# The output projection's bias: from a matrix product on TensorE to an addition on GpSimd

## The chip, the cores and the metric

The kernel runs on one core of a Trainium2 chip. A core has five engines, each with its own queue of instructions that it works off in order: TensorE (PE, matrix products; PEld is its loading of weights), VectorE (DVE), ScalarE (ACT), GpSimd (POOL) and SyncE (SP, which here issues the DMAs). PE writes to PSUM, eight banks of memory beside it; GpSimd works on SBUF, the main on-chip memory. The metric is the device time of one execution in microseconds (us), the median of several.

## The reference

Four sequences of 2048 tokens with 256 channels pass through four layers, each added to its input:

```python
x = x + _L0_attn_a_ref(_layernorm(x, axis=-1), ...)   # row 1 of the sequence times W, plus b, for all tokens
x = x + _L0_ffn_ref(_layernorm(x, axis=-1), ...)
x = x + _L0_attn_b_ref(_layernorm(x, axis=-1), ...)   # 16 heads of 64, window of 128 tokens back, RoPE
x = x + _L0_ffn_ref(_layernorm(x, axis=-1), ...)
```

The FFN is `sigmoid(xr @ W_r) * (relu(xk @ W_k)**2 @ W_v)`, where `xr` and `xk` mix each token with the one before it. The windowed attention ends in

```python
return merged @ Wo.T + bo
```

and it is this `bo`, 256 numbers that are the same for every token, that the change is about.

## The kernel before, in words

Tokens are worked off in 32 groups of 256 (`g`), two tiles `j` of 128 tokens each (128 partitions); eight groups make a sequence. A group passes through the stages load (`x`), first FFN (`f0`), normalisation for attention (`ln`), values (`v0` to `v3`), queries and keys of four quads of heads (`q0` to `q3`), attention of the four quads (`s0` to `s3`), output projection (`o`), second FFN (`f1`; the last group's is cut into two halves, `f1` and `f2`) and store (`sv`). A stage is a list of steps. Each line of such a list (`SPEC`, for instance lines 1127 to 1135) names a step, its engine (`p` PE, `v` DVE, `s` ACT, `g` POOL, `q` a DMA on SP) with an assumed duration, the steps it needs, the buffers it takes and the buffers it gives back.

A planner (`Plan`, line 143) turns these lists into one order before the program is built. It plays the steps through on the assumed durations; whenever an engine is free, it takes among the steps that could begin within 0.3 us of the earliest the one with the lowest rank. A rank is group times 44 plus a number from the table `RANK` (line 51), plus an extra number for the first five and the last five groups. The table's numbers come from a search. The order is fixed by this: the engines work off their queues as issued (`_Engine`, line 264, through whose line 276 nearly all instructions are recorded, so that most rows of the profile name that line). In the steady part, instructions of several groups stand mixed on each engine; while PE forms the first q product of one group, it finishes the output projection of the group three before it.

Values are split in a high and a low half, so that the products are exact enough in half-width numbers. For a product of tokens and weights three products run, high by high, high by low, low by high. What the change and the prediction touch:

- `Ln` (line 1126). The steps are `st` (mean and variance on DVE), `rs` (shift and scale on POOL, tiles `a_mv`, `a_rs`), `xn` (the normalised rows, on POOL, tile `a_xn`, from the tokens `x`), `hi` (ACT), `lo` (the low half, on POOL, `a_xhl`), `tr` (a transposing DMA on SP, `a_xT`). `a_xT` feeds the products for values, queries and keys.
- `Out` (line 1485). Each of `o0` and `o1` forms for one tile of 128 tokens 24 products of 128x256 (eight slices of the 1024 channels of the heads, three products each) from the transposed context (`at_ctT`) and the weights `WO`, and adds a 25th, `ones` by `bo3` (line 1513), all into one half of a PSUM bank (`po`). `ad` (for the last group the halves `b0`, `b1`) then runs on DVE: x = po * osc + x, where `osc` undoes the weights' scale.
- `bo3` (line 377) holds the scaled bias in three rows of bf16 numbers that sum to it, other rows zero, so that a product with a matrix of ones gives the bias on every row. The setup step `ob` (line 805) makes it by ten GpSimd instructions on three partitions, in the tile `tmp`. It comes after `mk`, which makes the attention mask's factors from the mask in the same tile; `lm` loads mask and bias into it.
- `Load` (line 924). Its step `a1` adds the first layer's result to the tokens on POOL (`x<-x,vb`), an instruction of 128x512 numbers.
- Setup (line 457) loads and rescales all weights, each with a few large products (`u_q`, `u_k`, `u_v`, `u_o`, sums of squares `pn_q`, `pn_k`, `pn_v`), among the first groups' first steps.

Of the kernel before, what the change touches and what calls it, by code (L numbers as in the profile page):

```python
# [8 lines left out]
BF16 = mybir.dt.bfloat16  # L9
# [9 lines left out]
P = 128  # L19
# [32 lines left out]
    "p.c1": -5056.91, "p.c2": 2969.02, "p.c3": -4885.05, "p.lv": -3111.05, "p.lb": -2925.83, "p.lw": -5009.81,  # L52
    "p.lo": -413.49, "p.lk": -2678.25, "p.lm": 2640.67, "p.lq": -3077.55, "p.fk": -1972.19, "p.fr": -2838.78,
    "p.fv": -777.00, "p.bd": -2779.47, "p.nvs": 3014.63, "p.nvm": 3072.90, "p.nvr": -2978.83, "p.nks": -788.22,
    "p.nkm": -4306.80, "p.nkr": -83.63, "p.nqs": -5037.35, "p.nqm": -4939.68, "p.nqr": -774.36, "p.sc": -472.11,
    "p.wv0": 570.16, "p.xv0": -201.89, "p.yv0": 3153.22, "p.zv0": -4686.76, "p.wv1": -2600.05, "p.xv1": -3342.91,
    "p.yv1": -610.29, "p.zv1": -4852.83, "p.wk0": -3021.86, "p.xk0": -1892.46, "p.yk0": -821.64, "p.zk0": -2369.83,
    "p.wk1": -2733.80, "p.xk1": -83.69, "p.yk1": -1953.56, "p.zk1": -2430.55, "p.wq0": -168.05, "p.xq0": 2297.47,
    "p.yq0": -4898.14, "p.zq0": -5081.41, "p.wq1": 2689.14, "p.xq1": -2913.52, "p.yq1": 3363.58, "p.zq1": -5071.63,
    "p.mk": -3071.43, "p.mu": -2906.24, "p.frh": -2530.67, "p.frl": -2423.55, "p.fkh": -2983.12, "p.fkl": 3185.31,  # L60
    "p.fvs": -769.81, "p.fvh": -4579.58, "p.fvl": 3091.15, "p.oq": -3006.79, "p.om": -204.90, "p.oc": -4648.57,
    "p.ox": -4580.42, "p.ob": -4965.08, "p.wo0": -613.03, "p.yo0": -2788.56, "p.zo0": -2882.62, "p.wo1": 3475.98,
    "p.yo1": -4703.07, "p.zo1": -4980.00, "r.ld": -5200.49, "r.st": 3455.58, "r.rs": -4687.73, "r.xn": 3456.91,
    "r.tr": 2907.19, "r.cp": -4814.90, "r.mm": 3513.18, "r.bi": -4976.56, "r.ad": -273.75, "x.ld": -4781.49,
    "x.a1": -513.94, "f0.st": -4882.63, "f0.rs": 2754.65, "f0.xn": 2986.21, "f0.tr": -4910.79, "f0.xt": -4990.79,
    "f0.hs": -3080.33, "f0.d": 2586.18, "f0.xm": -151.13, "f0.xo": -4611.65, "f0.xh": 976.57, "f0.xl": -4986.30,
    "f0.pk": -393.93, "f0.pr": -1868.76, "f0.rl": 3385.50, "f0.sq": 2308.38, "f0.kh": -5040.27, "f0.kl": -676.62,
    "f0.th": -6078.70, "f0.pv": 1034.70, "f0.sg": -4582.52, "f0.ad": 2796.64, "ln.st": -560.18, "ln.rs": -2135.71,
    "ln.xn": -358.88, "ln.hi": -845.47, "ln.lo": -4727.91, "ln.tr": -4597.42, "ln.cs": 1425.54, "tab.sc": 2955.10,
    "tab.st": -4548.65, "v0.mm": 1390.97, "v0.hi": -4851.14, "v0.lo": -952.76, "v1.mm": -2687.29,  # L70
    "v1.hi": -2644.64, "v1.lo": 2842.52, "v2.mm": 75.57, "v2.hi": -351.20, "v2.lo": -3081.42, "v3.mm": -4752.71,
    "v3.hi": -3057.25, "v3.lo": -4482.10, "q0.qm": -697.49, "q0.km": -1950.26, "q0.ka": -2699.89,
    "q0.kb": -5039.26, "q0.ad": 6.08, "q0.hi": -4974.92, "q0.lo": -5211.77, "q0.ks": -630.96, "q1.qm": -3584.31,
    "q1.km": -5189.02, "q1.ke": -5178.75, "q1.ka": -4943.18, "q1.mu": -992.72, "q1.ad": 1417.95, "q1.hi": 2888.04,
    "q1.lo": -4733.64, "q1.ks": -4326.00, "q2.qm": -468.39, "q2.km": -5058.89, "q2.ka": -2789.23,
    "q2.kb": -2972.37, "q2.ad": -2884.86, "q2.hi": 2658.83, "q2.lo": -924.24, "q2.ks": -2518.12, "q3.qm": 518.16,
    "q3.km": -4610.64, "q3.ka": 2530.62, "q3.kb": -4722.76, "q3.ad": -2764.39, "q3.hi": 2839.46, "q3.lo": -857.55,
    "q3.ks": -6086.78, "s0.k0": -1920.73, "s0.k1": -4586.15, "s0.k2": -613.21, "s0.k3": -2474.73,
    "s0.ks": -1923.23, "s0.sc": -3035.71, "s0.m0": -3099.45, "s0.m1": -3049.20, "s0.m2": -3015.22,
    "s0.m3": 2557.63, "s0.e0": -861.34, "s0.h0": -2876.34, "s0.l0": -2849.45, "s0.e1": 3370.73, "s0.h1": -2599.69,  # L80
    "s0.l1": 1349.23, "s0.t0": -2539.64, "s0.e2": 3083.70, "s0.h2": -1860.52, "s0.l2": 3055.36, "s0.e3": 2664.91,
    "s0.h3": -4879.42, "s0.l3": -610.50, "s0.t1": -4583.99, "s0.av": -4852.99, "s0.i0": 570.93, "s0.n0": -3079.20,
    "s0.ch": 2366.40, "s0.cl": -571.44, "s0.tc": -571.05, "s1.k0": -3309.12, "s1.k1": -1922.89, "s1.k2": -3002.20,
    "s1.k3": -2726.33, "s1.ks": -184.97, "s1.sc": -2823.37, "s1.m0": -2407.99, "s1.m1": -5176.15,
    "s1.m2": -1860.79, "s1.m3": 2664.46, "s1.e0": -2792.04, "s1.h0": -5036.68, "s1.l0": -5011.21,
    "s1.e1": -2759.97, "s1.h1": -2211.92, "s1.l1": -435.00, "s1.t0": -901.97, "s1.e2": 3228.18, "s1.h2": -2875.68,
    "s1.l2": -330.17, "s1.e3": -3095.98, "s1.h3": -4480.63, "s1.l3": -2400.51, "s1.t1": -40.32, "s1.av": -4976.07,
    "s1.i0": -302.67, "s1.n0": -5059.03, "s1.ch": -2945.71, "s1.cl": -4833.32, "s1.tc": -580.01, "s2.k0": -5104.06,
    "s2.k1": -2518.92, "s2.k2": -609.18, "s2.k3": -198.65, "s2.ks": -4270.64, "s2.sc": -3396.12, "s2.m0": -5359.90,
    "s2.m1": 3353.04, "s2.m2": -2954.66, "s2.m3": 2954.52, "s2.e0": -4801.17, "s2.h0": -4748.29, "s2.l0": -2533.65,  # L90
    "s2.e1": 2657.60, "s2.h1": -4876.22, "s2.l1": -143.77, "s2.t0": 3181.31, "s2.e2": -4740.23, "s2.h2": -1971.93,
    "s2.l2": -938.59, "s2.e3": 2929.40, "s2.h3": 3383.64, "s2.l3": -3250.26, "s2.t1": -4528.02, "s2.av": -3295.20,
    "s2.i0": -813.73, "s2.n0": -495.95, "s2.ch": -48.33, "s2.cl": 3091.26, "s2.tc": -696.74, "s3.k0": -677.40,
    "s3.k1": -3123.97, "s3.k2": -1933.84, "s3.k3": -465.00, "s3.ks": -4922.97, "s3.sc": -3446.85, "s3.m0": -798.61,
    "s3.m1": -4809.14, "s3.m2": 2876.12, "s3.m3": -4696.24, "s3.e0": -3417.38, "s3.h0": -4927.16,
    "s3.l0": -1999.52, "s3.e1": -4448.94, "s3.h1": -2880.18, "s3.l1": -280.82, "s3.t0": -2938.10,
    "s3.e2": -4878.66, "s3.h2": 3143.56, "s3.l2": -4964.39, "s3.e3": -4936.60, "s3.h3": -2514.89,
    "s3.l3": -1028.30, "s3.t1": -492.35, "s3.av": -2744.89, "s3.i0": 3016.46, "s3.n0": -1868.36, "s3.ch": 884.13,
    "s3.cl": -4564.07, "s3.tc": -5366.32, "o.o0": 2643.02, "o.o1": -3044.73, "o.ad": -158.89, "f1.st": 2937.82,
    "f1.rs": -2889.62, "f1.xn": 3469.38, "f1.tr": -4576.63, "f1.xt": 552.29, "f1.hs": -510.30, "f1.d": -2519.76,  # L100
    "f1.xm": 3150.42, "f1.xo": -608.94, "f1.xh": -2506.38, "f1.xl": -4708.72, "f1.pk": -1296.49, "f1.pr": 3476.81,
    "f1.rl": -5093.90, "f1.sq": -2850.79, "f1.kh": -5039.71, "f1.kl": -814.45, "f1.th": -3076.11, "f1.pv": 2685.28,
    "f1.sg": -2990.66, "f1.ad": -805.51, "sv.sv": -5172.96, "q0.kp": -272.05, "q1.kp": 3376.69, "q2.kp": -1225.68,
    "q3.kp": 3472.01, "o.b0": 1345.63, "o.b1": -2554.79, "w0.sv": 3471.29, "f2.st": -5011.19, "f2.rs": -3308.71,
    "f2.xn": -3405.13, "f2.tr": -2831.72, "f2.xt": -3325.07, "f2.hs": -2014.91, "f2.d": 1332.12, "f2.xm": 2950.21,
    "f2.xo": 2796.33, "f2.xh": 3364.00, "f2.xl": -909.62, "f2.pk": -2992.00, "f2.pr": 2885.42, "f2.rl": 539.64,
    "f2.sq": 1425.59, "f2.kh": -67.86, "f2.kl": 2844.93, "f2.th": 2905.43, "f2.pv": -5337.55, "f2.sg": 3157.44,
    "f2.ad": -4704.62, "w1.sv": 3214.41, "x!0": 280.61, "f0!0": -466.19, "ln!0": -1931.41, "tab!0": 407.32,
    "v0!0": -398.48, "v1!0": -330.74, "v2!0": -346.65, "v3!0": 347.03, "q0!0": -660.79, "q1!0": 28.80,
    "q2!0": 462.27, "q3!0": -379.97, "s0!0": 250.27, "s1!0": 1256.31, "s2!0": 655.38, "s3!0": -1508.73,  # L110
    "o!0": -1757.96, "f1!0": -2364.52, "sv!0": 2125.66, "x!1": -633.85, "f0!1": -1962.50, "ln!1": 1727.42,
    "tab!1": -240.15, "v0!1": -2055.69, "v1!1": -17.38, "v2!1": -1635.07, "v3!1": -1933.31, "q0!1": 1435.50,
    "q1!1": -913.86, "q2!1": 541.01, "q3!1": -1282.06, "s0!1": -1069.83, "s1!1": 856.98, "s2!1": -2363.56,
    "s3!1": -571.61, "o!1": 860.95, "f1!1": 519.89, "sv!1": -1291.03, "x!2": -877.71, "f0!2": -334.58,
# [1582 lines left out]
```

## Time and profile before

| what | value |
|---|---|
| median of 3 runs | 1600.59 us (1600.19 to 1601.61) |
| profiled execution, its own time | 1597.72 us |
| its span, first to last instruction | 1595.9 us |
| mean granted PE clock in it | 0.991 |
| DMA | 248.23 MB, mean 156 GB/s |
| x<-x,vb on POOL | 32, 1274 ns each |
| po<-bo,ones on PE | 64, 273 ns each, 17.4 us busy |

A row of the profile gives engine, operation, written tile <- read tiles, shape, count, then busy time and the mean duration of one in ns. Durations of products include the time until the result is through the array, and products overlap in it; how fast they follow each other is seen in a timeline, from start to start. In a timeline a row begins with start and duration in us, and ends with the time for which the engine stood idle before it and the engine and tile that it waited for. In a table by stage a row has the stretch, its length, each engine's busy time and count of instructions, the granted PE clock, the share of time that the DMA engines were busy, and GB/s.

The period of a steady group, from one group's last bias product to that of the next, is 46 to 47 us.

### The profile page before, as it was taken

The page shows a single profiled execution, that of the slowest core. Times are in us where ns is not written, and L with a number is a line of the kernel's source. Part 1 is how long each engine was busy: PE and PEld are TensorE (multiplying, and loading weights), DVE is VectorE, ACT ScalarE, POOL GpSimd, SP SyncE. Part 2 cuts the span into 40 slices and gives each one's busy share as a digit, 9 for nine tenths or more (in the row PEclk, how much of TensorE's full clock was granted, in tenths as well). Part 3 has the DMA queues.
Part 4 walks back from the last instruction along what each step waited for, and adds up shares of the span by engine and source line. Part 5 has one row for each costly group of instructions (what it writes and reads, how often), then busy time and mean ns, then how long its engine had stood idle before and what let it go on. Part 6 is the DMA issues. An engine that isn't in the chain of part 4 may idle for free.

```text
span 1595.9 us, 55776 instructions
## 1 busy us (share of the span) xinstructions
PE 1493.1 (94%) x22887; PEld 1241.3 (78%) x22888; DVE 1438.1 (90%) x2607; ACT 1345.6 (84%) x2742; POOL 1317.3 (83%) x1409
## 2 busy tenths in 40 slices
PE   7989889999999999999999999999999999999976
PEld 4767778777777887887887878788887778887765
DVE  6889898999999999999999999999999999998973
ACT  5678788888988888898988889898888989888882
POOL 6899877788888888888888889888888988888732
PEclk9999999999999999999999999999999999999997
DMA  7059998889889799989798989997878989989781
GB/s 225 11 131 168 163 175 179 153 167 157 148 160 173 164 153 163 160 170 161 159 152 152 166 165 166 169 168 166 139 149 152 181 155 173 163 164 161 147 159 34
DMA packets 858831, 248.23 MB, mean 156 GB/s; under 512 B 822736, under 2 KB 857808, under 8 KB 858576
## 3 DMA queue, kind: packets, MB, share of 16 engines
q1 hardware_dynamic: 858144, 244.66, 82.3%
q8 instruction: 179, 2.93, 0.8%
q14 instruction: 76, 0.62, 0.1%
q10 hardware_dynamic: 432, 0.01, 0.0%
HBM read 42.22 MB, written 26.21 MB: 43 GB/s over the span
## 4 chain that ended last, share of the span: by engine, by line
PE 52%; DVE 18%; ACT 17%; POOL 7%; issue 6%; DMA 1%; DVEq 0%; ACTq 0%; SPq 0%; POOLq 0%
PE qk_pd L276 11%; PE po L276 9%; PE at_s L276 8%; PE pv L276 7%; PE at_cx L276 7%; PE f_pv L276 5%; ACT at_s L276 5%; DVE qk_A L276 3%; ACT at_phl L276 3%; DVE at_phl L276 3%; DVE at_mn L276 3%; PE f_pk L276 3%; PE f_pr L276 2%; DVE qk_B L276 2%; ACT f_xh L276 2%
## 5 line engine op out<-in xcount | busy, mean ns | idle before, releaser
L276 ACT ACTIVATE at_s<-at_s,at_mn 128x256 f32<-128x256 f32 x1024 | 462.7, 452 | 27.7 <-DVE at_mn L276 11.0
L276 DVE TENSOR_TENSOR at_phl<-at_s,at_phl 128x512 f16<-128x512 f32 x512 | 346.3, 682 | 40.3 <-ACT at_phl L276 37.1
L276 POOL TENSOR_TENSOR qk_A<-qk_A,qk_B 128x512 f32<-128x512 f32 x256 | 320.9, 1277 | 44.9 <-DVE qk_B L276 43.9
L276 DVE TENSOR_REDUCE at_mn<-at_s 128x2 f32<-128x512 f32 x512 | 325.3, 680 | 3.5 <-PE at_s L276 3.2
L276 ACT CAST at_phl<-at_s 128x512 f16<-128x512 f32 x512 | 300.6, 587 | 12.8 <-DMA at_pt<-at_phl 0.4
L276 PE MATMUL at_cx<-v,at_pt 128*128 128x65 f16 x5952 | 202.6, 194 | 37.3 <-DVE qk_B L276 24.5
L276 PEld LDWEIGHTS <-at_pt 128*128 128x128 f16 x5952 | 193.8, 98 | 52.0 <-issue 48.3
L276 POOL TENSOR_TENSOR at_ct<-at_c,at_ct 128x512 f16<-128x512 f32 x128 | 149.0, 1164 | 63.0 <-ACT at_ct L276 62.7
L276 PE MATMUL at_s<-qk_k,qk_q 32*128 32x256 f16 (+1 forms) x6144 | 189.7, 264 | 0.0
L276 PE MATMUL qk_pd<-a_xT,w_q_h 128*128 128x256 f16 x1024 | 176.3, 274 | 9.3 <-DVE at_c L276 3.8
L276 POOL TENSOR_TENSOR f_xl<-f_xm,f_xh 128x1024 fp32r<-128x1024 f32 x63 | 148.7, 2360 | 40.0 <-issue 24.9
L276 PE MATMUL po<-wo_h,at_ctT 128*128 128x256 f16 x1024 | 178.0, 273 | 1.0 <-DMA at_ctT<-at_ct 1.0
L276 DVE TENSOR_TENSOR qk_A<-qk_pd,a_cs 128x1024 f32<-128x1024 f32 x128 | 156.0, 1219 | 23.6 <-PE qk_pd L276 10.1
L276 PE MATMUL qk_pd<-a_xT,w_k_h 128*128 128x256 f16 x1024 | 176.8, 275 | 0.0
L276 PE MATMUL pv<-w_v_h,a_xT 128*128 128x512 f16 x512 | 161.7, 379 | 12.2 <-DVE at_phl L276 9.4
L276 PEld LDWEIGHTS <-at_ctT 128*128 128x128 f16 x1536 | 147.9, 98 | 18.1 <-DMA at_ctT<-at_ct 1.2
L276 PEld LDWEIGHTS <-qk_q 32*128 32x128 f16 x6144 | 153.4, 93 | 6.1
L276 POOL TENSOR_TENSOR qk_k<-qk_A,qk_k 128x512 f16<-128x512 f32 x128 | 149.4, 1167 | 0.0
L276 POOL TENSOR_TENSOR qk_q<-qk_A,qk_q 128x512 f16<-128x512 f32 x128 | 149.3, 1166 | 0.0
L276 PEld LDWEIGHTS <-a_xT 128*128 128x128 f16 x768 | 71.3, 98 | 98.9 <-DVE at_phl L276 16.9
L276 PE MATMUL qk_pd<-a_xT,w_k_l 128*128 128x256 f16 x512 | 140.6, 275 | 0.0
L276 PE MATMUL qk_pd<-a_xT,w_q_l 128*128 128x256 f16 x512 | 140.1, 274 | 0.0
(195 smaller groups left out, 3866.6 us busy)
## 6 DMA issues: line engine op xcount, KB each, us to landing
qk_kd<-qk_k SPq DMA_DIRECT2D x112, 128.0 KB, 2.4
qk_k<-qk_kd SPq DMA_DIRECT2D x112, 128.0 KB, 3.1
a_cs<-csd SPq DMA_DIRECT2D x24, 384.0 KB, 3.8
x<-in_x_dram SPq DMA_DIRECT2D x32, 256.0 KB, 3.6
out_dram<-x SPq DMA_DIRECT2D x31, 256.0 KB, 2.5
at_pt<-at_phl SPq DMA_TRANSPOSE x256, 4.5
a_cs<-in_cs_dram SPq DMA_DIRECT2D x32, 96.0 KB, 3.4
csd<-a_cs SPq DMA_DIRECT2D x8, 384.0 KB, 3.2
```

What stands on the lines that cost most here:

```text
L276: ins = fn(*a, **k)
```

## The change

The bias no longer passes through PE. The 25th product of each half goes (its predecessor closes the sum), with `bo3` and the setup step `ob`. The bias is loaded by a step of its own (`lx`) onto all 128 partitions (`bo_sb`), and the mask alone into a smaller `tmp`. In each group a new GpSimd step, `bo`, adds it to the tokens in SBUF once `xn` has read them; the rest of the stage uses the normalised rows, not the tokens. The final addition in `Out` (`ad`, `b0`) now needs this step.

```diff
-    bo3 = cp.tile([P, C], BF16, name="bo3")
+    bo_sb = cp.tile([P, 1, C], F32, name="bo_sb")
...
         def lm(self):
-            W["tmp"] = work("pt", [P, 4, C], F32, "tmp")
-            self.bo = W["tmp"][:, 1, :]
-            nc.sync.dma_start(self.bo, bo.rearrange("(o c) -> o c", o=1).broadcast_to([P, C]))
-            self.mask = W["tmp"][:, 0, :]
+            self.mask = work("pt", [P, C], F32, "tmp")
             nc.sync.dma_start(self.mask, mask)
+
+        def lx(self):
+            nc.sync.dma_start(bo_sb[:, 0, :], bo.rearrange("(o c) -> o c", o=1).broadcast_to([P, C]))
...
         xn g 1.06 | rs    | xn>xn   | mv rs
+        bo g 1.24 | xn p:lx |       |
         hi s .52  | xn    | xhl>x   |
...
+        def bo(self):
+
+            x = XT[self.g]
+            nc.gpsimd.tensor_tensor(x, x, bo_sb.broadcast_to([P, GB, C]), op=ALU.add)
...
-        o0 p 2.72 | s0:tc s1:tc s2:tc s3:tc p:zo0 p:zo1 p:ob | pp>po |
-        o1 p 2.72 | o0           |        | s0:u s1:u s2:u s3:u
+        o0 p 2.62 | s0:tc s1:tc s2:tc s3:tc p:zo0 p:zo1 | pp>po |
+        o1 p 2.62 | o0           |        | s0:u s1:u s2:u s3:u
...
-        ad v .79  | o1           |        | po
+        ad v .79  | o1 ln:bo     |        | po
...
-                    stop=False,
+                    stop=(n == 23),
                 )
-            nc.tensor.matmul(PO[self.g][:, j, :], ones, bo3, start=False, stop=True)
```

All numbers of `RANK` are replaced by those of a new search, so the order of nearly every queue differs somewhere. In the steady part the differences are small. On POOL the group's sequence was `xn`, a quad's `cl` (at_ct), `f1.rs`, `lo`, `q2.lo` (the pair qk_q, qk_k), `q3.ad` (qk_A), and so on; it is now `xn`, `bo`, `cl`, `f1.rs`, `q2.lo`, `lo`, `q3.ad`, and from there as before. PE keeps its sequence of products but for the 25th ones. DVE changes places of a few neighbours (the second FFN's statistics, a quad's value halves), and ACT casts one quad's q and k before the normalised rows. The order of setup and of the first and the last groups differs more. SP's first loads were first row, w_a, tokens 0, w_v, b_a, w_q, w_r, tokens 1, w_k, ...; they are now w_a, first row, w_q, w_k, FFN w_v, mask, b_a, w_o, tokens 0, w_v, ... On PE, after the last group's last scores, there stand now also the products of the output projection of group 30 and the FFN products of group 29, which stood before them.

## The prediction

> **What bounds the kernel now.** I read the page first (busy shares, then the chain of waits), then busy time by stage, then the timeline of one group of tokens.
>
> ```profile
> PE 1493.1 (94%) x22887; PEld 1241.3 (78%) x22888; DVE 1438.1 (90%) x2607; ACT 1345.6 (84%) x2742; POOL 1317.3 (83%) x1409
> ...
> PE 52%; DVE 18%; ACT 17%; POOL 7%; issue 6%; DMA 1%; DVEq 0%; ACTq 0%; SPq 0%; POOLq 0%
> PE qk_pd L276 11%; PE po L276 9%; PE at_s L276 8%; PE pv L276 7%; PE at_cx L276 7%; PE f_pv L276 5%; ACT at_s L276 5%; DVE qk_A L276 3%; ACT at_phl L276 3%; DVE at_phl L276 3%; DVE at_mn L276 3%; PE f_pk L276 3%; PE f_pr L276 2%; DVE qk_B L276 2%; ACT f_xh L276 2%
> ```
>
> PE is the fullest engine and carries half of the chain; the products into po, from which the change takes some, are 9% of it. POOL, which gets the new work, is 7%. By stage (setup, filling, 1280 us of steady groups, emptying, the last wait):
>
> ```profile
> core 0: us, PE busy (x) PEld busy (x) DVE busy (x) ACT busy (x) POOL busy (x), PEclk, DMA share, GB/s
> ...
> 11.40:63.66 52.26, 51.48 (x282) 34.94 (x282) 44.40 (x115) 34.43 (x71) 39.98 (x71) 1.00 0.39 124
> 63.66:200.00 136.34, 122.14 (x1796) 98.47 (x1795) 116.45 (x194) 109.44 (x220) 122.27 (x122) 0.97 0.71 137
> 200.00:1480.00 1280.00, 1230.45 (x19502) 1033.23 (x19499) 1199.58 (x2148) 1126.19 (x2300) 1102.83 (x1143) 1.00 0.88 162
> 1480.00:1545.80 65.80, 58.62 (x1077) 48.70 (x1074) 56.44 (x103) 54.50 (x112) 37.80 (x36) 1.00 0.83 151
> 1545.80:1595.90 50.10, 28.68 (x238) 24.79 (x238) 19.38 (x44) 17.70 (x39) 10.88 (x17) 0.79 0.30 57
> ```
>
> PE idles 0.8 us in setup, 14.2 while the pipeline fills, 49.6 in the steady groups (4%), 7.2 and 21.4 at the end. In the steady part POOL has 14% to spare, DVE 6%. So PE sets the pace, with DVE close behind.
>
> **The change, part by part.** *The bias products go.* Their pitch is read off three starts in the PE timeline:
>
> ```profile
> 809.31 0.27 PE L276 MATMUL po<-wo_h,at_ctT 128*128 128x256 f16 x1
> ...
> 809.42 0.27 PE L276 MATMUL po<-bo,ones 128*128 128x256 bf16 x1
> ...
> 809.53 0.60 PE L276 MATMUL f_pt<-ident,f_xn 128*128 128x128 f32 x4
> ```
>
> One takes its place for 0.11 us (0.27 is latency; 25 products of one half take 2.73 us in the chain, 0.109 each). There are 2 per group, 64 in all: 64 x 0.109 = 7.0 us of PE. How much lies on the path? The chain gives po 9% of 1595.9 = 144 us; all po work is 32 x 2 x 2.73 = 175 us. So 0.82 of it is on the path: 5.7 us gained. Ends: 7.0 if all of it is, 0 if DVE's waits fill the room.
>
> *GpSimd adds the bias, 32 times.* The row of the same form is the first add, x<-x,vb, 128x512 f32, 1274 ns: 32 x 1.27 = 40.8 us on POOL, which rises from 83% to about 85%. Whether this shows is a matter of place. The add stands straight after the normalised rows; behind it in POOL's queue are a head's ct (at_ct), an FFN's f_rs, and the low half of the normalised rows (a_xhl). The new order also moves the pair qk_q, qk_k ahead of a_xhl. One group before:
>
> ```profile
> 814.32 1.10 POOL L276 TENSOR_SCALAR a_xn<-x,a_rs 128x256 f32<-128x256 f32 x2
> 816.02 1.16 POOL L276 TENSOR_TENSOR at_ct<-at_c,at_ct 128x512 f16<-128x512 f32 x1 [0.59 <-ACT at_ct L276]
> 817.82 0.22 POOL L276 TENSOR_SCALAR f_mv<-f_mv 128x2 f32<-128x2 f32 x1 [0.64 <-DVE f_mv L276]
> ...
> 819.38 1.16 POOL L276 TENSOR_TENSOR a_xhl<-a_xn,a_xhl 128x512 f16<-128x512 f32 x1
> 820.50 1.17 POOL L276 TENSOR_TENSOR qk_q<-qk_A,qk_q 128x512 f16<-128x512 f32 x1
> 821.62 1.18 POOL L276 TENSOR_TENSOR qk_k<-qk_A,qk_k 128x512 f16<-128x512 f32 x1
> 823.76 2.52 POOL L276 TENSOR_TENSOR qk_A<-qk_A,qk_B 128x512 f32<-128x512 f32 x2 [0.96 <-DVE qk_B L276]
> ```
>
> The add runs 815.42 to 816.69; at_ct starts 0.67 late, f_mv about 0.05 (its own wait takes up the rest), the pair takes 2.26, so a_xhl is 2.3 us late. The same sum in the next group, where the waits are 0.16 and 0.64, gives 2.8. By 823.76 POOL waits for DVE anyway, so queue and add end there: the cover is these three waits, 2.2 us here, 1.27 without them. What is late next is a_xhl's transpose on SP's queue and the first q product:
>
> ```profile
> 820.57 1.23 SPq L276 DMA_TRANSPOSE a_xT<-a_xhl  x1
> ```
>
> ```profile
> 826.96 0.39 PE L276 MATMUL qk_pd<-a_xT,w_q_h 128*128 128x256 f16 x2
> ```
>
> The transpose lands a median 3.1 us after issue (here at 823.5), so PE had 3.4 us to spare. Over the 20 groups 7 to 26 I read 2.1 to 4.3, median 3.3. A delay of 2.3 to 2.8 fits, barely; four groups have less than 2.8 and together lose 1.6 at most. I take +0.5. If no wait absorbs anything the delay is 1.27 + 2.26 = 3.53, and the shortfalls add up to 7.5 us over those 20 groups, 9.7 over 26: the upper end. The final add to x waits for the new step too, but that is three groups earlier: nothing.
>
> *Setup.* The ten small GpSimd steps that split the bias go: from 38.19 until the next work at 45.80.
>
> ```profile
> 38.19 0.47 POOL L276 TENSOR_SCALAR tmp<-tmp,small 3x256 f32<-3x256 f32 x1
> ...
> 45.80 0.24 POOL L276 TENSOR_SCALAR f_mv<-f_mv 128x2 f32<-128x2 f32 x1
> ```
>
> The chain runs through them, but I value these 7.6 us at nothing: PE's own setup products cover them (idle 0.8 us from 11.4 to 63.7), so 0.8 is the most they can give. Against that, the first loads are reordered: the mask, once fourteenth step on SP's queue, is sixth, the bias gets its own load (same 128 KB), and w_v falls behind w_o and the first tokens. Ahead of and with w_v stand about 5.2 MB; at the 244 GB/s of the first 11.4 us it lands near 22. Its squares take 2.1 us on ACT (sq_v, 2 x 1057 ns), so PE can begin the sums for v near 24. PE's new order puts before them the row work (to 12.2), the sums for q and k (2 x 1.3), half of q (5.3) and of w_o (1.8): 21.9. I take +2. Ends: -0.8, and +7 if the first four adds (5.1 us) also hurt between 63.7 and 200, where POOL is 90% busy.
>
> *The emptying.* New ranks move PE work. From the last scores (end 1545.8) to the last po (1568.3) lie 22.5 us, with PE mostly waiting. The new order holds back until there one at_cx, both po halves of group 30 and an FFN's pk, pr, pv: 1.5 + 5.3 + 0.4 + 4.3 = 11.4 us. DVE and ACT carry 56.4 and 54.5 us of the 65.8 before it and lose about 6 of them; at the same fullness that stretch shortens by 8 to 9. But group 30's FFN now starts later, and its xl (2.36) stands before the last head's ct on POOL; I count 3 to 5 us lost. I take -4; ends -9 and +3.
>
> [...]
>
> *Sum*, on the profiled execution (span 1595.9, time 1597.72): -5.7 + 0.5 + 2 - 4 = -7.2, so span 1588.7, time 1590.5. The median 1600.59 is 2.87 above that execution: 1593.4, I say **1593**.
>
> **Rivals.** *More is gained*: all 7.0 of PE, setup's 0.8, emptying's 9 with no delay: 1583.8 at the best; I give 1586. For it: PE is continuous in the steady chain. Against: the late loads.
>
> *PE's room is filled*: DVE, 94% busy in the steady part, is what PE waits for there (25.7 us of waits of at_cx on qk_A and qk_B), so 0.22 us less per group becomes 0.22 more waiting: 0 + 0.5 + 2 - 2.5 = 0, hence 1600.6. Against: the chain stays on PE through po for whole half-groups.
>
> *Slower: the late transpose.* One mechanism: a_xhl comes more than 3.3 us late, PE stands before the first q product of most groups. 9.7 us lost, with -5.7, +2 and no gain in the emptying: +6, so 1606.6. It decides from a delay of 3.3 us. For it: 1.27 + 2.26 exceeds that. Against: the waits on POOL.
>
> That the change does less than it says has no place: the new order has 64 products fewer and 32 adds more.
>
> **How the numbers follow.** Forecast 0.50, more 0.16, filled room 0.16, slower 0.18. What a measurement can tell from no change is about 0.2%, 3.2 us: 1597.4 and 1603.8. Of the forecast (own range 1587 to 1599) 0.42 lies below 1597.4; with 0.16, 0.06 and 0.02 from the others faster is 0.66; same 0.15, slower 0.19. The range 1584 to 1604 leaves out most of the slower rival and the best case.
>
> **What would show it.** Right: no po<-bo rows, a POOL row x<-x,bo_sb near 1.27 us, po pitch unchanged, PE's idle time in the steady part still near 50 us, landings of a_xT still ahead of the first q product by 0.3 to 1 us, PE idle near 22 to 24 us, fewer than 28.6 us idle in the last 115. Wrong: PE waiting for a_xT or for DVE more than before by over 6 us; a first q product later than 66 us; a last stretch not shorter.

## The result, and the profile after

The changed kernel takes 1606.41 us (median of 7 runs, 1603.35 to 1607.88) against 1601.61 us for the kernel before (7 runs, 1600.19 to 1603.81): ratio 1.0026, 95% interval 1.0015 to 1.0038. It is slower by 4 to 5 us, where the forecast was 7 us faster. The profiled execution took 1604.99 us, span 1603.0.

From its page, busy shares and the chain of waits:

```profile
PE 1496.1 (93%) x22823; PEld 1241.0 (77%) x22824; DVE 1441.7 (90%) x2606; ACT 1344.4 (84%) x2742; POOL 1349.6 (84%) x1431
...
PE 46%; POOL 17%; DVE 14%; ACT 13%; issue 6%; DMA 2%; SPq 0%; ACTq 0%; DVEq 0%; POOLq 0%
PE qk_pd L276 9%; PE at_s L276 7%; PE at_cx L276 7%; PE po L276 7%; PE pv L276 6%; ACT at_s L276 4%; POOL qk_A L276 4%; ACT at_phl L276 3%; DVE at_phl L276 3%; PE f_pv L276 3%; DVE qk_A L276 3%; PE f_pk L276 3%; DVE qk_B L276 2%; POOL x L276 2%; DVE at_mn L276 2%
```

PE has 64 products fewer and yet is 3 us busier, over a longer span; POOL's share of the chain went from 7% to 17%. The add itself, among POOL's groups, and what PE waited for between 200 and 1480 us for the transposed rows:

```profile
L276 POOL TENSOR_TENSOR x<-x,bo_sb 128x512 f32<-128x512 f32 x32 | 41.0, 1280 | 2.5
```

```profile
PE qk_pd L276 <- DMA a_xT<-a_xhl: 0.6, 1, 0.6
```

The add costs what it was priced at (1280 ns, forecast 1.27 us), and PE waited 0.6 us, once, for the transpose that it makes late. Neither explains a loss. A table by stage does. A stage border is taken where DVE adds the projection of a group (5, 24, counted from 0), at the last scores' end, and at the last instruction:

| span of the stage, us | before | changed |
|---|---|---|
| start to group 5's add (setup and filling) | 394.1 | 399.2 |
| group 5's to group 24's add (19 steady groups) | 882.5 | 877.6 |
| group 24's add to the end of the last scores | 269.2 | 265.6 |
| end of the last scores to the end | 50.2 | 60.5 |

The steady groups gain 4.9 us. Filling loses 5.1 and the emptying 6.7 (319.4 to 326.1), together 11.8. Each column is one execution; the two are 7.0 us apart in span, where the medians are 4.8 apart. The clock is little of the emptying's loss: after the last scores PE is at half clock for 21.3 us in the kernel before and for 21.2 us in the changed one, ahead of them for 3.4 us (from 1435.0 us) in the changed one alone. The emptying in the table by stage, first of the kernel before, then of the changed kernel (length, then busy time of PE, PE's weight loads, DVE, ACT, POOL, granted clock, DMA share, GB/s):

```profile
1276.55:1417.95 141.40, 136.65 (x2194) 115.60 (x2191) 133.01 (x242) 123.50 (x253) 123.61 (x132) 1.00 0.89 162
1417.95:1500.74 82.79, 80.00 (x1308) 65.62 (x1307) 75.54 (x126) 72.67 (x151) 68.15 (x66) 1.00 0.90 163
1500.74:1545.76 45.02, 39.25 (x756) 34.56 (x756) 38.03 (x71) 37.14 (x76) 20.09 (x18) 1.00 0.87 154
1545.76:1568.32 22.56, 12.04 (x137) 10.96 (x137) 9.73 (x19) 11.68 (x23) 7.14 (x8) 0.77 0.53 91
```

```profile
1276.88:1420.33 143.45, 135.50 (x2204) 114.26 (x2201) 133.85 (x238) 126.66 (x259) 129.15 (x131) 1.00 0.95 166
1420.33:1522.32 101.99, 92.56 (x1523) 74.52 (x1523) 89.15 (x156) 84.37 (x173) 72.37 (x72) 0.98 0.83 148
1522.32:1542.50 20.18, 19.56 (x384) 16.92 (x384) 17.09 (x31) 17.16 (x36) 12.02 (x14) 1.00 0.94 146
1542.50:1574.87 32.37, 24.00 (x272) 21.78 (x273) 16.19 (x33) 17.57 (x35) 11.88 (x11) 0.89 0.68 121
```

The borders of the first rows lie at group 27's add and at the last q product, of the last row at the last po. PE is busy for 24.0 us between the last scores and the last po, where it was 12.0: the work is held back, as forecast. But the stretch ahead of the last scores, relieved of it, shrank only from 269.2 to 265.6. In it PE idles 18.0 us (7.95 + 9.43 + 0.62) in place of 13.3. Added up over the three rows, DVE's work fell by 6.5 us (246.6 to 240.1) and ACT's by 5.1 (233.3 to 228.2), both by more than the length did: the tail of the pipeline runs thinner.

### The profile page after: what moved, and what is told of

Read it like the earlier page. It is cut to its first block, busy times and chain, and to the rows that moved or that the text cites. A ratio compares the mean times of both kernels' runs of the same rounds, so it can differ in the third digit from the quotient of the medians.

```text
span 1603.0 us, 55628 instructions
## 1 busy us (share of the span) xinstructions
PE 1496.1 (93%) x22823; PEld 1241.0 (77%) x22824; DVE 1441.7 (90%) x2606; ACT 1344.4 (84%) x2742; POOL 1349.6 (84%) x1431
## 4 chain that ended last, share of the span: by engine, by line
PE 46%; POOL 17%; DVE 14%; ACT 13%; issue 6%; DMA 2%; SPq 0%; ACTq 0%; DVEq 0%; POOLq 0%
PE qk_pd L276 9%; PE at_s L276 7%; PE at_cx L276 7%; PE po L276 7%; PE pv L276 6%; ACT at_s L276 4%; POOL qk_A L276 4%; ACT at_phl L276 3%; DVE at_phl L276 3%; PE f_pv L276 3%; DVE qk_A L276 3%; PE f_pk L276 3%; DVE qk_B L276 2%; POOL x L276 2%; DVE at_mn L276 2%
## 5 line engine op out<-in xcount | busy, mean ns | idle before, releaser
L276 ACT ACTIVATE at_s<-at_s,at_mn 128x256 f32<-128x256 f32 x1024 | 462.4, 452 | 39.8 <-DVE at_mn L276 19.8
L276 DVE TENSOR_TENSOR at_phl<-at_s,at_phl 128x512 f16<-128x512 f32 x512 | 346.5, 683 | 29.4 <-ACT at_phl L276 26.4
L276 POOL TENSOR_TENSOR qk_A<-qk_A,qk_B 128x512 f32<-128x512 f32 x256 | 320.8, 1275 | 40.3 <-DVE qk_B L276 37.8
L276 DVE TENSOR_REDUCE at_mn<-at_s 128x2 f32<-128x512 f32 x512 | 326.9, 681 | 6.2 <-PE at_s L276 4.8
L276 ACT CAST at_phl<-at_s 128x512 f16<-128x512 f32 x512 | 300.2, 586 | 12.3 <-DMA at_pt<-at_phl 0.2
L276 PE MATMUL at_cx<-v,at_pt 128*128 128x65 f16 x5952 | 202.4, 194 | 41.7 <-DVE qk_B L276 27.6
L276 PEld LDWEIGHTS <-at_pt 128*128 128x128 f16 x5952 | 192.8, 98 | 58.0 <-issue 54.6
L276 PE MATMUL at_s<-qk_k,qk_q 32*128 32x256 f16 (+1 forms) x6144 | 191.7, 265 | 0.0
L276 PE MATMUL qk_pd<-a_xT,w_q_h 128*128 128x256 f16 x1024 | 176.5, 274 | 13.6 <-DVE at_c L276 4.1
L276 DVE TENSOR_TENSOR qk_A<-qk_pd,a_cs 128x1024 f32<-128x1024 f32 x128 | 156.5, 1222 | 34.3 <-PE qk_pd L276 18.8
L276 POOL TENSOR_TENSOR at_ct<-at_c,at_ct 128x512 f16<-128x512 f32 x128 | 148.9, 1163 | 40.2 <-ACT at_ct L276 34.3
L276 POOL TENSOR_TENSOR f_xl<-f_xm,f_xh 128x1024 fp32r<-128x1024 f32 x63 | 148.6, 2359 | 37.4 <-issue 21.5
L276 PE MATMUL po<-wo_h,at_ctT 128*128 128x256 f16 x1024 | 176.9, 273 | 0.0
L276 PE MATMUL qk_pd<-a_xT,w_k_h 128*128 128x256 f16 x1024 | 176.5, 274 | 0.0
L276 PE MATMUL pv<-w_v_h,a_xT 128*128 128x512 f16 x512 | 162.3, 379 | 5.4 <-DVE at_phl L276 2.4
L276 PEld LDWEIGHTS <-at_ctT 128*128 128x128 f16 x1536 | 148.0, 98 | 17.3 <-issue 0.4
L276 POOL TENSOR_TENSOR qk_q<-qk_A,qk_q 128x512 f16<-128x512 f32 x128 | 148.8, 1162 | 14.8 <-ACT qk_q L276 14.6
L276 PEld LDWEIGHTS <-qk_q 32*128 32x128 f16 x6144 | 155.2, 93 | 6.3 <-issue 0.4
L276 POOL TENSOR_TENSOR qk_k<-qk_A,qk_k 128x512 f16<-128x512 f32 x128 | 148.9, 1163 | 0.0
L276 PE MATMUL qk_pd<-a_xT,w_k_l 128*128 128x256 f16 x512 | 140.5, 274 | 0.0
L276 PEld LDWEIGHTS <-a_xT 128*128 128x128 f16 x768 | 71.8, 98 | 88.6 <-issue 5.3
L276 PE MATMUL qk_pd<-a_xT,w_q_l 128*128 128x256 f16 x512 | 140.3, 274 | 0.0
```

Source lines behind the costliest of these rows:

```text
L276: ins = fn(*a, **k)
```

## The experiments

Two theories stood against each other, and a third beside them. *Theory*: the change alone is worth about 5 us, and the new order of issue at the two ends gave them back. *Rival 1*: GpSimd's add costs them. *Rival 2*: the products were worth nothing, and the steady part gained by the new ranks. To part change and order, the order of issue was written out in the kernel in place of the planner's:

```diff
-    for fn in plan.order():
-        fn()
+    for key in ORDER:
+        plan.ops[key][2]()
```

"Old order" is the list that the planner makes for the kernel before, without `p.ob`, with `p.lx` behind `p.lm` and `ln.bo` behind `ln.xn`. All ratios below are against the kernel before, timed beside each run; intervals are 95%, and the difference of two of them is uncertain by some 2.5 us.

| run | median us | ratio | interval |
|---|---|---|---|
| changed kernel | 1606.41 | 1.0026 | 1.0015 to 1.0038 |
| changed_again | 1605.07 | 1.0034 | 1.0022 to 1.0046 |
| old_order_with_change | 1596.57 | 0.9978 | 0.9967 to 0.9988 |
| old_order_no_products | 1594.15 | 0.9961 | 0.9947 to 0.9975 |
| old_order_add_late | 1595.93 | 0.9967 | 0.9955 to 0.9979 |
| new_order_products_kept | 1610.47 | 1.0065 | 1.0049 to 1.0081 |
| new_order_no_add | 1602.98 | 1.0023 | 1.0011 to 1.0034 |
| old_head_new_rest | 1601.79 | 1.0007 | 0.9995 to 1.0018 |
| new_then_old_tail | 1598.55 | 0.9987 | 0.9975 to 0.9999 |
| new_order_tail_moves | 1602.14 | 1.0010 | 0.9997 to 1.0023 |
| new_order_head_moves | 1603.80 | 1.0027 | 1.0016 to 1.0038 |
| old_order_best | 1590.28 | 0.9932 | 0.9919 to 0.9944 |
| before_with_moves | 1595.49 | 0.9962 | 0.9949 to 0.9976 |

**The change without its order.**

> The change in the order of the kernel before: every engine issues as before, with the products by ones gone, the bias loaded behind the mask, and GpSimd's add right behind the normalised rows of each group. Theory (the change is worth about 5 us and the new order at both ends gave them back): 4 to 6 us faster than the kernel before, about 1596, PE idle after the last scores near 20 us. Rival 1 (the add itself costs, by a late transpose or a fuller GpSimd at the ends): within 2 us of the kernel before or slower, 1600 to 1606. Rival 2 (the products were worth nothing): 1600 to 1602.

Measured 0.9978: 3.5 us faster than the kernel before (1.9 to 5.3), and 0.0048, 7.7 us, below the changed kernel. Nearest to the theory, just under its size; PE idle after the last scores is 20.8 us, as expected. The chain goes back to what it was:

```profile
PE 53%; DVE 16%; ACT 16%; POOL 8%; issue 6%; DMA 1%; ACTq 0%; DVEq 0%; POOLq 0%; SPq 0%
```

POOL's 17% in the changed kernel is thus not the add's: the same 32 adds are here, and POOL is at 8%.

**The products back in the new order.**

```diff
-                    stop=(n == 23),
+                    stop=False,
                 )
+            nc.tensor.matmul(PO[self.g][:, j, :], ones, bo3, start=False, stop=True)
```

> The changed kernel with the 64 products put back at their old places on TensorE, against a matrix of zeros, so that the output stays that of the changed kernel; order and add are untouched. Theory: each product lengthens the chain by 0.8 of its 0.109 us, 5 to 6 us slower than the changed kernel, about 1612, or 10 us slower than the kernel before. Rival 1: the same. Rival 2 (the products are worth nothing, the steady part gained by the new ranks): as the changed kernel, 1606.

Measured 1.0065, 5.0 to 6.2 us above the two measurements of the changed kernel. Rival 2 falls. Only a part of this is in the steady groups: in the profiles the 19 of them take 879.3 us with the products and 877.6 without.

**The add taken away in the new order.**

```diff
-            nc.gpsimd.tensor_tensor(x, x, bo_sb.broadcast_to([P, GB, C]), op=ALU.add)
```

> The changed kernel without GpSimd's add, so the output lacks the bias of the output projection; order otherwise untouched. Theory: the add is hidden by the 2 to 4 us that the transpose has to spare, and takes little at the ends: 0 to 2 us faster than the changed kernel, 1604 to 1606. Rival 1: the add costs what the products gave, so 5 us or more faster than the changed kernel, below 1601.

Measured 1.0023, 0.5 to 1.8 us below the changed kernel. Rival 1 wanted 5 or more, and falls.

**The products taken away in the old order.** The kernel before without the line of the 25th product.

> The kernel before without its 64 products by ones and nothing in their place, so the output lacks the bias of the output projection; the setup of the bias stays. Theory: 5 to 6 us faster than the kernel before, about 1596, and within 1 us of the run that has the add in the same order. Rival 1: as much as the theory, but the run with the add stands 5 us above it. Rival 2: no change, 1600 to 1602.

Measured 0.9961, 6.2 us faster. The run with the add stands 0.0017, 2.7 us, above it, more than the theory's 1 us and less than rival 1's 5; with the add behind `lo` (below) it is 1.0 us. Both are within the uncertainty of a difference.

**Which end.** The order was spliced from the two lists:

```diff
+i = OLD.index("o.ad@8")      # new_then_old_tail: NEW.index("o.ad@20"), and the lists swapped
+ORDER = OLD[: i + 1] + [k for k in NEW if k not in OLD[: i + 1]]
```

> The changed kernel, issued in the old order until the residual add of group 8 and in the new order from there, so only the filling is the old one. Theory (new order costs about 4 us in the filling and 6 in the emptying): 4 us faster than the changed kernel, so 0 to 1 us above the kernel before. Rival (the new order's loss is all in the emptying, and the filling differs only by where the clock happened to drop): as the changed kernel, 4 to 5 us above the kernel before.

> The changed kernel, issued in the new order until the residual add of group 20 and in the old order from there, so only the emptying is the old one. Theory: 6 us faster than the changed kernel, so 1 to 2 us below the kernel before. Rival (the emptying only shows a loss that comes from earlier, and the last groups end late whatever their order): within 2 us of the changed kernel.

Measured 1.0007 and 0.9987. Against 1.0026 the old filling gives back 3.0 us and the old emptying 6.2 (4.3 and 7.5 against the repeat's 1.0034); the sum of the first two, 9.2, is somewhat more than the 7.7 between the two whole orders. The stages of the profiles agree for the emptying: 326.1 us from group 24's add in the changed kernel, 324.8 with the new order after group 8, 318.3 with the old one after group 20, 319.9 in the old order throughout.

**Inside the emptying.** What PE waited for after the last scores, among its instructions in the changed kernel:

```profile
1564.85 0.39 PE L276 MATMUL f_pk<-f_xh,fw_k_h 128*128 128x256 f32 x1 [1.96 <-ACT f_xh L276]
...
1567.27 0.39 PE L276 MATMUL f_pk<-f_xl,fw_k_h 128*128 128x256 f32 x1 [1.92 <-POOL f_xl L276]
...
1572.87 0.39 PE L276 MATMUL f_pv<-fw_v_h,f_kh 128*128 128x256 f32 x1 [1.22 <-ACT f_kh L276]
...
1574.87 0.28 PE L276 MATMUL po<-wo_h,at_ctT 128*128 128x256 f16 x1
```

and POOL beside it:

```profile
1564.87 2.35 POOL L276 TENSOR_TENSOR f_xl<-f_xm,f_xh 128x1024 fp32r<-128x1024 f32 x1 [1.12 <-ACT f_xh L276]
1567.18 1.17 POOL L276 TENSOR_TENSOR at_ct<-at_c,at_ct 128x512 f16<-128x512 f32 x1
```

The last projection (po) stands behind group 30's whole FFN on PE, and the last context's low part (at_ct) behind that FFN's f_xl on POOL. Moves that turn this round:

```diff
 TensorE:  s3.av@31 f1.pk@30
-f1.pr@30 f1.pv@30 o.o0@31 o.o1@31
+o.o0@31 o.o1@31 f1.pr@30 f1.pv@30
 GpSimd:
-f1.xl@30 s3.cl@31 f1.ad@30 f1.rs@31 f2.rs@31
+s3.cl@31 f1.xl@30 f1.rs@31 f2.rs@31 f1.ad@30
 ScalarE:  f1.th@30 behind f1.kh@30;  VectorE:  f1.sg@30 behind f2.st@31
```

> The changed kernel in its new order with a few steps of the last two groups moved: on GpSimd the last context's low part ahead of f_xl of group 30, on TensorE the last output projection ahead of group 30's products for f_pr and f_pv, and what hangs on these (f_th on ScalarE, the last steps of group 30 on VectorE and GpSimd) behind. Theory: the last output projection begins 4 to 5 us sooner (1570 us in place of 1574.9), and the kernel is 4 us faster than the changed one, about the time of the kernel before. Rival (the last projection waits for its transposed context, not for the products ahead of it): no change.

Measured 1.0010, 2.6 us below the changed kernel. The last po begins 28.7 us after the last scores, not 32.4; it could have been sooner, but f_pk, left ahead of it, now waited 3.50 us for f_xl. So the moves are worth some 3 us, but this queueing is not what parts the two orders: in the kernel before, too, the last po stands behind group 30's f_pk, f_pr and f_pv, and the last at_ct behind its f_xl. What parts them is where group 30's FFN begins. Its first product in the kernel before:

```profile
1558.39 0.58 PE L276 MATMUL f_pk<-f_xh,fw_k_h 128*128 128x256 f32 x1 [3.73 <-ACT f_xh L276]
```

That is 12.6 us after the last scores (12.9 in old_order_with_change). In the changed kernel it is 22.4 (1564.85, the first row under this heading) and with the moves 22.3, since group 30's projection and group 29's FFN now come after the last scores; DVE adds that projection 8.5 us after them, where it was 3.3 us ahead of them. From this first product to the last po it is 9.9 us before and 10.0 in the changed kernel, from the last po to the end 27.6 and 28.1. So nearly all of the 10.3 us by which the wait grew lie ahead of that one product. The splices agree: with the old emptying it comes 12.8 us after the last scores, which are followed by 50.4 us in all; with the old filling and the new emptying 22.3 and 60.5. Against old_order_with_change the new order is 2.1 us shorter from group 24's add to the last scores (265.6 to 267.7) and 8.3 us longer from there to the end (60.5 to 52.2), with the moves still 5.2.

**The add's place.** `ln.bo` behind `ln.lo` in all groups of the old order:

> The change in the old order, as in the run old_order_with_change, but GpSimd's add stands behind the low part of the normalised rows and not ahead of it, so that the transpose of every group is issued 1.27 us sooner. Theory (in the steady part the transpose has 2 to 4 us to spare and the add costs nothing; in the first three groups TensorE waits for it): 0 to 2 us faster than old_order_with_change, 1594.5 to 1596.5. Rival (the late transpose costs in every group): 5 us or more faster, below 1592.

Measured 0.9967, 1.8 us below old_order_with_change: as the theory had it, though not beyond the uncertainty. The 19 steady groups take 878.8 us with the add late, 879.1 with it early, 879.3 without add: there it is free. In the new order, where `q2.lo` also stands ahead of `lo`, an early add is not free: 877.6 early, 875.9 late, 876.0 without.

**Inside the filling.** On POOL the first row's statistics stand behind a cast that waits for the biases of q, k and v (first kernel: the changed one; the idle time ahead is the last number):

```profile
7.85 0.23 POOL L276 TENSOR_TENSOR small<-small 128x24 bf16<-128x24 f32 x1 [5.20 <-DMA small<-in_bv_dram]
...
8.53 0.23 POOL L276 TENSOR_SCALAR xb0mv<-xb0mv 128x1 f32<-128x1 f32 x1
```

```diff
 GpSimd:
-p.bd r0.rs ... ln.xn@g ln.bo@g ... ln.lo@g
+r0.rs p.bd ... ln.xn@g ... ln.lo@g ln.bo@g
```

> The changed kernel once more, untouched, beside the runs that follow, for the size of its loss and of the spread of its filling. Theory: 4 to 5 us above the kernel before, 1605 to 1606; last scores to the end 60.5 us again, since that order repeats, while the time at which group 5 adds its projection moves by some 3 us from the 399.2 us of the first profile, with the stretches in which the granted clock is below 1. Rival (the filling's loss is as fixed as the emptying's): 399.2 within 1 us.

> The changed kernel in its new order with two moves on GpSimd: the statistics of the first row (r0.rs) ahead of the cast that waits for the biases of q, k and v (p.bd), and the add of every group behind the low part of its normalised rows. Theory (the filling lost 1.1 us where TensorE's first product waited behind those biases, and 1.3 us of the 3.17 us that it waits for the first transposed rows are the add): first product near 9 us in place of 10.2, the wait ahead of the first product for q near 2 us, 2 to 3 us faster than the changed kernel, 1 to 3 us above the kernel before. Rival (the setup is bound by its weights, not by its first product): 0 to 1 us faster than the changed kernel.

The repeated kernel gave 1.0034 and group 5's add at 400.1 us, within 1 us of the first profile, as its rival had it; from the last scores to the end it took 61.1 us, expected 60.5. The moves gave 1.0027: 1.1 us below it, where 2 to 3 were expected. The first product came at 9.32 us in place of 9.65 beside it and 10.22 in the first profile, the wait ahead of the first product for q was 2.59 us in place of 3.20 and 3.17. That is the rival's size: the setup is not bound there. Which steps of the new filling cost its 3 us stays open; the largest single difference in the profiles is from group 1's add to group 2's, 54.4 us in the changed kernel and 49.2 in old_order_with_change, but part of it is gained elsewhere.

**A version that beats both.** The old order with the add late, r0.rs first, and in the emptying:

```diff
 TensorE:
-f1.pk@30 s3.av@31 f1.pr@30 f1.pv@30 o.o0@31 o.o1@31
+s3.av@31 f1.pk@30 f1.pr@30 o.o0@31 o.o1@31 f1.pv@30
 ScalarE:  s3.ch@31 ahead of f1.rl@30
 VectorE:  f1.sg@30 behind f2.st@31;  GpSimd:  f1.ad@30 behind f2.rs@31
```

> The change in the old order with the add behind the low part, the first row's statistics ahead of the cast of the biases, and in the emptying the last context's products and its cast ahead of group 30's f_pk on TensorE and its steps on ScalarE, and the last output projection ahead of group 30's f_pv. Theory: the last context begins at about 1555 us in place of 1559.9 as counted in old_order_with_change, the last projection begins 2 us sooner and runs without its 0.8 us wait, so 2 to 4 us faster than old_order_add_late: 1592 to 1594, some 8 us below the kernel before. Rival (the last context's transposed weights land only shortly before 1559.9): as old_order_add_late, 1596.

Measured 0.9932: 10.9 us below the kernel before. In old_order_with_change the last context's products stood behind f_pk, which waited 1.63 us for f_xl, and began at 1559.87; here they begin 8.6 us sooner (7.3, counted from the last scores) and run while f_xl is made (L869 is in this longer kernel what L276 is elsewhere):

```profile
1551.26 1.48 PE L869 MATMUL at_cx<-v,at_pt 128*128 128x65 f16 x24 [1.19 <-DVE at_c L869]
1552.89 1.50 PE L869 MATMUL at_cx<-v,at_pt 128*128 128x65 f16 x24 [0.16 <-DMA at_pt<-at_phl]
```

They waited 0.16 us for the transposed weights: those land when they are wanted, so the rival falls too. The last run parts the moves from the change:

> The kernel before, products by ones and all, with the same moves as old_order_best and no add on GpSimd: it parts the change from the moves. Theory (the moves and the change add up): the moves are worth 5 to 6 us, so 1595 to 1596 or 0.9965 of the kernel before, and the change 4 to 5 us of the 11 that old_order_best gained. Rival (the moves only pay because the bias's own steps are gone from GpSimd and TensorE): within 2 us of the kernel before.

Measured 0.9962. The moves alone give 6.1 us, the change on top 0.0030, 4.8 us. They add up.

## Why the prediction was wrong

**The bias products, -5.7: right, but not everywhere in the way it was put.** In the old order, 19 steady groups take 882.5 us with the products (882.5 again in before_with_moves), 879.1 without them but with the add, and 879.3 without both: 3.2 to 3.4 us for 38 products, 0.085 to 0.090 each, 5.4 to 5.7 for 64. Taking the products away there gave 6.2 us of whole time, so the share of 0.82 read off the chain held. The rival that DVE's waits fill the room falls for the old order: over the 19 groups PE idles 32.8 us with the products and 33.4 without, so 0.6 of their 4.1 us were filled. In the new order it is in part right: there the 38 products make only 1.7 us (879.3 and 877.6), and without them PE idles 31.4 us in place of 29.2. That putting them back nevertheless cost 5.0 to 6.2 us of whole time is not explained by the steady groups.

**GpSimd's add, +0.5: the delay right, its cost too small.** In the changed kernel a_xhl came as late as forecast. POOL in one group, the add and what follows:

```profile
955.29 1.10 POOL L276 TENSOR_SCALAR a_xn<-x,a_rs 128x256 f32<-128x256 f32 x2
956.47 1.29 POOL L276 TENSOR_TENSOR x<-x,bo_sb 128x512 f32<-128x512 f32 x1
...
960.43 1.16 POOL L276 TENSOR_TENSOR qk_q<-qk_A,qk_q 128x512 f16<-128x512 f32 x1
961.54 1.17 POOL L276 TENSOR_TENSOR qk_k<-qk_A,qk_k 128x512 f16<-128x512 f32 x1
962.67 1.18 POOL L276 TENSOR_TENSOR a_xhl<-a_xn,a_xhl 128x512 f16<-128x512 f32 x1
```

8.6 us from a_xn's start to a_xhl's end, where the sum on record started from 6.2: 2.3 us late. The transpose landed at 968.15 and the first product for q came at 968.30. Over groups 7 to 26 it landed a median 1.5 us ahead of that product (3.3 in the kernel before), at the least 0.14. Measured, the add costs 1.6 us over the 19 steady groups of the new order (877.6 less 876.0), nothing in the old one, and 0.5 to 2.7 us of whole time. PE's one wait for the transpose is 0.6 of the 1.6; where the rest goes was not traced. The rival "late transpose" gave 1606.6, near the result, but for a reason that did not happen: PE waited 0.6 us for the transpose, not 9.7. The right number from the wrong mechanism is no support for it.

**Setup and filling, +2: size within its ends, mechanism wrong.** It measured 3.0 us by the splice (4.3 against the repeat). The late w_v that was to cost it cost nothing: its last part landed at 20.40 us, and PE's sums for v began at 23.79 us with no gap ahead of them. PE waited instead for its first product (to 10.22 us, before 9.14), 3.17 us for the first transposed rows and 1.5 us for the second group's; in the kernel before it waits for no transposed rows there. How much of the 3.0 us is theirs stays open: with the first two shortened and the third gone, new_order_head_moves gained 1.1 us.

**The emptying, -4: this step failed, in both of its terms.** It put: "at the same fullness that stretch shortens by 8 to 9", and behind it "I count 3 to 5 us lost".

The first term: DVE and ACT lost about the 6 us of work that it names (6.5 and 5.1), but the fullness did not stay the same. The stretch shortened by 3.6 us, and against the old order with the same change by only 2.1, while PE idled more in it (18.0 us for 13.3). That a chain through several engines sets the length, and not the work of any one of them, is the likely reason; it was not tested by itself. The sum was off as well: at the fullness of its row (DVE 56.4 of 65.8 us), 6 us of work are 7.0 us of time, not 8 to 9.

The second term: group 30's FFN does start later, as it says, but by 9.7 us and not 3 to 5, and the wait after the last scores grew by 10.3 (by 8.3 against the old order with the same change). The f_xl ahead of the last at_ct, which it counts as a cost, stood there before as well. Nor was PE "mostly waiting" in that wait: it was busy for 12.0 of the 22.6 us, so the 12.0 us of work held back found little room.

Together that is +6.7 in the profiles of the two kernels, +6.2 against the old order with the same change and +6.2 by the splice, outside both ends (-9 and +3). The prediction's own sign of being wrong, "a last stretch not shorter", showed. PE's idle time did fall as forecast after 1480 us (28.6 to 22.9), and it meant nothing, since the span grew: idle time of the bounding engine is a good measure only when its work stays where it was.

**DVE's pace beside GpSimd's add, nothing in the sum: right.** In the kernel before, DVE's scaling of xb, 128x256 f32, took 412 ns with POOL idle and 1389, 908 and 1201 ns while a POOL step ran; at_phl, 128x512, stayed at 635 to 693 ns in all 512. What the 32 adds do to DVE is seen in the old order: it is busy for 1438.1 us in the kernel before, without them, and for 1436.6 in old_order_with_change, with them. Had each add held DVE up for its whole length, that would be 32 x 1.28 = 41 us more.

**The sum.** With the measured sizes: -5.7 for the products, +0.5 to +2.7 for the add, +3.0 for the filling's order, +6.2 for the emptying's: +4.0 to +6.2. The changed kernel is 4.2 to 5.4 us slower. Each of these sizes but the first is a difference of ratios, uncertain by some 2.5 us, so that they add up this well is in part luck.

## What to carry to other kernels

A change that comes with a new search of the order is two changes, and they can have opposite signs: write the old order out by hand, put the change alone into it, and measure it before judging either. Here the edit was worth 3.5 to 4.8 us and its new order cost 8 to 9. When work is held back past a point, ask which engine's chain sets the time ahead of that point, and what will start later behind the held-back work: here one group's FFN began 9.7 us later, and nearly the whole loss of the emptying was in that. The last item of a pipeline should go ahead of what nobody waits for; such moves gained 2.6 us in the new order and 6.1 in the kernel before.

## What the runs showed of the hardware

The same wait can cost PE its clock, or not. Busy time and granted clock (the number before the last two) at the wait for the first transposed rows, in the changed kernel and in new_order_tail_moves, whose order is the same there:

```profile
61.85:65.02 3.17, 0.00 (x0) 0.03 (x1) 2.95 (x7) 3.11 (x8) 0.16 (x1) 1.00 0.37 83
65.02:66.40 1.38, 1.38 (x13) 1.20 (x14) 0.80 (x3) 1.38 (x3) 0.54 (x1) 0.96 0.00 0
66.40:69.00 2.60, 2.60 (x14) 1.92 (x13) 0.00 (x0) 0.37 (x1) 1.81 (x1) 0.50 0.00 0
```

```profile
62.62:65.82 3.20, 0.00 (x0) 0.03 (x1) 2.97 (x7) 3.14 (x8) 0.18 (x1) 1.00 0.36 82
65.82:67.20 1.38, 1.38 (x13) 1.24 (x14) 0.80 (x3) 1.38 (x3) 0.54 (x1) 1.00 0.00 0
67.20:69.80 2.60, 2.60 (x25) 2.48 (x24) 1.16 (x2) 0.36 (x1) 1.82 (x1) 1.00 0.00 0
```

After a gap of 3.2 us PE got half its clock in the one (14 products in 2.6 us) and all of it in the other (25 products). In the records of the kernel before and of the changed kernel the clock is at half for 3.41 us or two, three or four times that (but for the last stretch, which the end of the span cuts), 28.1 and 31.4 us in all of the two executions, all of it in the filling and the emptying.

Every change of the clock in these two records lies within 4 ns of a multiple of 3413.3 ns from the first entry. Cut at these multiples, the two have 911 stretches at full clock, of which 13 were followed by half clock. In those 13 PE was busy for 0 to 44% of the stretch, in the other 898 for 46% and more. The gap in the changed kernel above fell mostly into one stretch (62.86 to 66.28 us, PE busy for 37% of it), and the next was at half clock. These are counts of two profiles; no run varied a gap to see what sets the clock.

A shorter gap was enough elsewhere. One of 1.92 us in the kernel before (from 83.92 us) left its stretch 44% busy, and the clock was at half from 86.45 us; the stretch from 113.76 us was 46% busy, and the clock stayed whole. A stage with gaps scatters from run to run: with the changed kernel's filling, group 5's add came at 399.2, 400.1, 396.8 and 403.2 us in four profiles, in the first with 6.8 us at half clock ahead of it. The clock goes with such scatter: of the 23 executions of the kernel before that were timed beside old_order_with_change, the five with a mean granted clock of 0.990 or more took 1596.3 to 1597.6 us, the twelve with 0.986 or less 1600.9 to 1602.9. How much of the filling's scatter it makes was not shown. The 19 steady groups took 877.3 to 877.6 us in the three that keep its order so far. A difference of 3 us in the filling can't be read from one profile; one of 1 us in the steady part can.
